# Dequantised feed-forward weights turned by VectorE's 32x32 block transpose instead of TensorE

## The chip, the cores and the metric

The kernel runs on one core of one Trainium2 chip. The metric is the time of one execution on the device in microseconds (us). An execution of the kernel before took 3075.28 us (median of 3 runs, 3073.91 to 3076.26).

## The reference

The program is a chain of four transformer blocks on `x` of shape (8, 128, 512). Each block adds an attention and then a feed-forward to the residual, each behind a layer norm:

```
x = x + L0_xattn(layernorm(x), ctx, ...)    x = x + L0_ffn(layernorm(x), ...)
x = x + L1_xattn(layernorm(x), ctx, ...)    x = x + L1_ffn(layernorm(x), ...)
x = x + L2_xattn(layernorm(x), ctx, ...)    x = x + L2_ffn(layernorm(x), w1, w2, w3)
x = x + L3_xattn(layernorm(x), ctx, ...)    x = x + L3_ffn(layernorm(x), ...)
```

The change concerns the third feed-forward, whose weights are first rounded to the 16 values of NF4 in blocks of 64 (w1 and w2 are 1376 x 512, w3 is 512 x 1376):

```
def nf4_quant_dequant(w):
    flat = w.reshape(-1, 64)
    absmax = max(abs(flat), axis=1)
    idx = searchsorted(bounds, flat / where(absmax == 0, 1, absmax))
    return (NF4_CODE[idx] * absmax).reshape(shape)
dq1, dq2, dq3 = (nf4_quant_dequant(w) for w in (w1, w2, w3))
h = silu(x @ dq1.T) * (x @ dq2.T)
return h @ dq3.T
```

None of this depends on `x`, so the rounding can be done at any time before that feed-forward. A matmul on TensorE sums over the 128 partitions, so the kernel needs w1 and w2 with their 512 columns on the partitions, and w3 with its 1376 columns there. In memory all three have them along a row; they have to be turned.

## The kernel before

Tokens are handled in 8 batches of 128, in two halves of four batches. TensorE (PE) multiplies, VectorE (DVE) and ScalarE (ACT) do the elementwise work, GpSimd (POOL) some of it, and SyncE's queue (SP) issues most DMAs. SP issues in order: a DMA that waits for its data, for a free buffer or for an earlier DMA holds up all DMAs behind it.

The first 1860 us are a loop over 128 attention *units* (heads times halves): 64 of the first attention (`Unit0`), then 64 of the third (`Unit2`). A unit projects keys and queries (L252), takes scores (L280) and a softmax, turns the probabilities, weighs the values (L297) and adds the output projection (L218, L219). The probabilities are turned by `blocks_turned` (L233): a VectorE transpose of 32x32 blocks within each quarter of the partitions (L240), a store of the result to DRAM (L242) and four loads that put the blocks in place (L245). Scores and turning run two units ahead of the weighing, projections three. Weights come on the SP queue into a pool of 20 buffers.

Beside the units runs side work, in `slot()` (L1145), which is called after each projection and at a few more points. A slot runs what a table holds for it (the first half's and second half's layer norms, the whole of the first feed-forward, the second attention and the second feed-forward: the *short stages*), and then so many *pieces* of the NF4 work as the rate allows:

```
NF4_PACE = ((2.1, 2.1), (0.9, 2.2), (0.2, 1.6), (1.6, 1.6))
...
due[0] += 0.0 if turning[0] else NF4_PACE[stage[0]][0 if table else 1]
```

The stage is the unit's number divided by 32; the second rate of a pair holds when the table is empty. On VectorE a piece is queued behind the last marked operation of the attention. A scheduler then settles the order of instructions on each engine from the order in which they are written and its own estimate of when each is ready.

The NF4 work is a generator over chunks of at most 128 x 512 elements (`nf4_items`). A `yield` ends a piece. `Rows` takes 128 rows of w1 or w2 (the last chunk 96): load, block maxima (L772), scaling (L776), 15 rounding steps, each a ScalarE activation (L739) and a VectorE operation (L748, L750), and scaling back (L780). w3 has 1376 = 21.5 blocks of 64 in a row, so blocks straddle rows: `PairMax` takes pairs of rows and finds the maxima (L809), and `Pairs` rounds the same pairs, 256 columns of each row at a time (scaling L837, once for each row of the pair). Each chunk is turned in the middle of the next one, by `turn`: up to four PE transposes into PSUM (L787 for `Rows`, L856 for `Pairs`), a ScalarE copy out (L789, L859) and stores to DRAM tensors `d1`, `d2`, `d3` (L790, L860). The third feed-forward, `l2_ffn`, loads its weights from these (about 1870 to 2100 us), and the fourth block follows.

`layernorm` (L174) normalises a batch; its last operation is L183. The result is turned on PE (L190) and copied to `xT`, the input of projections.

Of the kernel before, what the change touches and what calls it, by code (L numbers as in the profile page):

```python
# [11 lines left out]
F32 = mybir.dt.float32  # L12
# [11 lines left out]
P = 128  # L24
# [38 lines left out]
def kernel(ctx: ExitStack, tc: tile.TileContext, a, out):  # L63
# [107 lines left out]
    neg2 = keep.tile([P, B, P], BF16, name="neg2")  # L171
    cs = [keep.tile([P, 2, 512], F32, name=f"cs{hf}") for hf in range(2)]

    def layernorm(st, b):  # L174
        stats = st.small(6, "st")
        V.bn_stats(stats, x[b])
        mv = st.small(2, "mv")
        V.bn_aggr(mv, stats)
        rs = st.small(1, "rs")
        V.tensor_scalar(rs, mv[:, 1:2], 1e-5, None, ALU.add)  # L180
        inv_sqrt(rs, [P, 1])
        h = st.wide("h")
        V.tensor_scalar(h, x[b], mv[:, 0:1], rs, ALU.subtract, ALU.mult)  # L183
        return h

    def transposed(st, src):
# [566 lines left out]
    def nf4_scales(ri, am):  # L753
# [2 lines left out]
        V.tensor_add(ri, ri, am)  # L756
        V.reciprocal(ri, ri)

    class Rows:

        def __init__(self, name, dst, hc):
            self.name, self.dst, self.hc, self.n = name, dst, hc, min(P, FF - hc * P)

        def load(self):
            self.w = nfp.tile([P, 512], F32, tag="nw", name="nw")
            load(self.w[:self.n], a[self.name][self.hc * P:self.hc * P + self.n, :])

        def work(self):
            n, w = self.n, self.w
            wb = w.rearrange("p (k e) -> p k e", e=64)[:n]  # L770
            am = nfp.tile([P, 8], F32, tag="am", name="am")
            V.tensor_reduce(am[:n], wb, AX.X, ALU.max, apply_absolute_value=True)  # L772
            ri = nfp.tile([P, 8], F32, tag="ri", name="ri")
            nf4_scales(ri[:n], am[:n])
            yield
            V.tensor_tensor(wb, wb, along(ri[:n], 64), ALU.mult)  # L776
            yield
            dq = nfp.tile([P, 512], F32, tag="dq", name="dq", bufs=1)
            yield from nf4_round(dq[:n], w[:n])
            V.tensor_tensor(wb, dq.rearrange("p (k e) -> p k e", e=64)[:n], along(am[:n], 64), ALU.mult)  # L780
            yield

        def turn(self, st):
            n, hc = self.n, self.hc
            tp = st.tp()
            for c in range(DC):
                T.transpose(tp[:, c, :n], self.w[:n, c * P:(c + 1) * P], ident[:n, :n])  # L787
            wt = nfp.tile([P, 4, P], F32, tag="wt", name="wt", bufs=1)
            S.copy(wt[:, :, :n], tp[:, :, :n])  # L789
            nc.sync.dma_start(self.dst[:, :, hc * P:hc * P + n], wt[:, :, :n])  # L790

    class PairMax:
        def __init__(self, c, k):
# [7 lines left out]
        def work(self):  # L803
            k, nb = self.k, self.nb
            if k == 0:
                pair["am"] = nfp.tile([P, 43, 2], F32, tag="am3", name="am3", bufs=1)
            am = pair["am"]
            wb = self.w.rearrange("p (k e) -> p k e", e=64)[:, :nb, :]
            V.tensor_reduce(am[:, k:k + nb, 0], wb, AX.X, ALU.max, apply_absolute_value=True)  # L809
            yield  # L810
            if k + nb == 43:
                V.tensor_copy(am[:, :, 1], am[:, :, 0])
                ri = nfp.tile([P, 86], F32, tag="ri3", name="ri3", bufs=1)
                amf = am.rearrange("p k t -> p (k t)")
                nf4_scales(ri, amf)
                pair["amr"] = amf.rearrange("p (r k) -> p r k", r=2)
                pair["rir"] = ri.rearrange("p (r k) -> p r k", r=2)
                yield

        def turn(self, st):  # L820
            pass

    class Pairs:
        def __init__(self, c, hc):
            self.c, self.hc, self.nw = c, hc, min(2 * P, FF - hc * P)

        def load(self):
            nw, hc = self.nw, self.hc
            self.w = nfp.tile([P, 512], F32, tag="nw", name="nw")
            load(self.w[:, :2 * nw].rearrange("p (r h) -> p r h", r=2),  # L830
                 a["L2_ffn_w3"].rearrange("(c p r) h -> c p r h", c=2, r=2)[self.c, :, :, hc * P:hc * P + nw])

        def scale(self, dst, src, f):
            ks = slice(self.hc * 4, self.hc * 4 + self.nw // 32)
            for r in range(2):
                d, s = (t[:, r * self.nw:(r + 1) * self.nw].rearrange("p (k e) -> p k e", e=32) for t in (dst, src))
                V.tensor_tensor(d, s, along(f[:, r, ks], 32), ALU.mult)  # L837

        def work(self):
            w, nw = self.w, self.nw  # L840
            self.scale(w, w, pair["rir"])
            yield
            dq = nfp.tile([P, 512], F32, tag="dq", name="dq", bufs=1)
            yield from nf4_round(dq[:, :2 * nw], w[:, :2 * nw])
            self.scale(w, dq, pair["amr"])
            yield

        def turn(self, st):
            nw, hc, c = self.nw, self.hc, self.c
            tp = st.tp()  # L850
            wt = nfp.tile([P, 4, P], F32, tag="wt", name="wt", bufs=1)
            ns = [min(P, nw - j) for j in range(0, nw, P)]
            for i, n in enumerate(ns):
                for r in range(2):
                    o = r * nw + i * P
                    T.transpose(tp[:n, 2 * i + r, :], self.w[:, o:o + n], ident)  # L856
            for i, n in enumerate(ns):
                wd = wt[:n, 2 * i:2 * i + 2, :].rearrange("p r q -> p (r q)")
                S.copy(wd.rearrange("p (q r) -> p r q", r=2), tp[:n, 2 * i:2 * i + 2, :])  # L859
                nc.sync.dma_start(d3[hc + i, :n, c * 2 * P:(c + 1) * 2 * P], wd)  # L860

    pair = {}

    def nf4_items(st):
        chunks = [Rows(name, dst, hc) for name, dst in (("L2_ffn_w1", d1), ("L2_ffn_w2", d2)) for hc in range(NHC)]
        for c in range(2):
            chunks += [PairMax(c, k) for k in range(0, 43, 8)]
            chunks += [Pairs(c, hc) for hc in range(0, NHC, 2)]
        chunks[0].load()
        for k, chunk in enumerate(chunks):  # L870
            lag = 0 if isinstance(chunk, PairMax) else 5
            for i, _ in enumerate(chunk.work()):
                if i == lag:
                    if k > 0:
                        chunks[k - 1].turn(st)
                    if k + 1 < len(chunks):
                        chunks[k + 1].load()
                yield
        chunks[-1].turn(st)


    def l2_ffn(st, hf, f2, xT):
# [219 lines left out]
    with ExitStack() as early:  # L1102
# [24 lines left out]
        def put(i, f, *args):  # L1127
            table.setdefault(i, []).append((f, args))

        items = nf4_items(side)  # L1130
        now, due = [0], [0.0]

        def slot():
# [12 lines left out]
            while table:  # L1146
                slot()

        def norm_pieces(i, box, b, get):

            def norm():
                box[b] = layernorm(side, b)

            def turn():
                S.copy(get()[:, :, cols(b)], transposed(side, box[b]))

            put(i, norm)
            put(i + 1, turn)
# [114 lines left out]
        for u, unit in enumerate(units):  # L1273
            stage[0] = u // (4 * NG)
            turning[0] = 8 * NG - 4 <= u < 8 * NG
            if u == 3:
                l0_half(1)
            if u in (4 * NG - 3, 8 * NG - 3, 12 * NG - 3):
                drain()
            if not unit.far:  # L1280
                unit.turn()
            if u + 3 < len(units):
                for f in units[u + 3].pieces():
                    f()
                    slot()
            if u + 2 < len(units):
                units[u + 2].score()
                if units[u + 2].far:
                    units[u + 2].turn_far()
            unit.weigh()  # L1290
            if isinstance(unit, Unit2):
                slot()
            unit.after(units, u)
            if u in (4 * NG - 1, 8 * NG - 1):
                short_stages((u + 1) // (4 * NG) - 1)
            if u == 12 * NG + 1:
                now[0] = 0
                xT.append(xt_tile())
                for b in batches(0):
                    norm_pieces(2 * b, {}, b, lambda: xT[0])  # L1300
        for _ in items:
            pass
    ps = ctx.enter_context(tc.tile_pool(name="ps2", bufs=1, space=PSUM))
# [2 lines left out]
    xT.append(xt_tile())  # L1306
    xT3 = []

    def late_norm(b, get):
        box = {}  # L1310
        return [lambda: box.setdefault("h", layernorm(late, b)),
                lambda: S.copy(get()[:, :, cols(b)], transposed(late, box["h"]))]

    with tc.tile_pool(name="f2", bufs=2) as f2:
        extra = [f for b in batches(1) for f in late_norm(b, lambda: xT[1])]
        for _ in l2_ffn(late, 0, f2, xT[0]):
            if extra:
                extra.pop(0)()
# [166 lines left out]
```

## Time and profile before

| what | value |
|---|---|
| time, median of 3 runs | 3075.28 us (3073.91 to 3076.26) |
| time of the profiled execution | 3075.35 us |
| its span in the profile | 3073.6 us, mean granted PE clock 0.998 |
| busy: PE, DVE, ACT, POOL | 3041.6, 1876.2, 1373.3, 384.4 us |
| DMA | 427.42 MB, 139 GB/s in the mean |
| NF4 chunk loads by SP | 46, first at 14.4 us, last at 1746.9 us |
| PE transposes of chunks | 88 (L787) and 44 (L856), 99.3 to 1795.5 us |

The span is one execution, from the first to the last instruction that the hardware profiler recorded. Busy time is the time in which an engine had an instruction running. PE's matmuls are pipelined: the next one starts before the end of the one before, so the time that a matmul costs is read from the distance of starts, and its listed duration is longer. PEld is PE's loading of the stationary operand, which overlaps. A group line reads: line, engine, operation, output from inputs, sizes, count | busy us, mean ns of one | idle time of the engine just before, and what ended it.

### The profile page before, as it was taken

The numbers are of one execution on the slowest core, as the hardware profiler recorded it, in microseconds if no ns is written. First come the engines' busy times: TensorE is split into PE (matmuls) and PEld (weight loads), VectorE is DVE, ScalarE is ACT, GpSimd is POOL, SyncE is SP. The second block draws the span as 40 slices with busy tenths as digits, with TensorE's granted clock in tenths as the row PEclk, the third lists the DMA queues.
The fourth block names the chain that finished last, engine by engine and source line by source line (L and its number), as shares of the span: only waits on it lengthen the run. The fifth ranks groups of instructions, "written<-read, shape, count | busy, mean of one in ns | idle before, by whom it ended". The sixth has DMA issues, their size and how long they took to land.

```text
span 3073.6 us, 35109 instructions
## 1 busy us (share of the span) xinstructions
PE 3041.6 (99%) x10720; PEld 1668.8 (54%) x10724; DVE 1876.2 (61%) x3765; ACT 1373.3 (45%) x3856; POOL 384.4 (13%) x490
## 2 busy tenths in 40 slices
PE   9999999999999999999999999999999999999999
PEld 4555555544444565555555554445656656555554
DVE  5666666657766566898889862214554555555544
ACT  4555555435654433665556641003343433433332
POOL 2000000101211021332111110001111111111110
PEclk9999999999999999999999999999999999999999
DMA  6434343336654533665344342223565645655540
GB/s 216 127 113 120 120 134 116 110 100 181 177 157 126 153 111 92 179 188 171 117 139 129 122 121 77 78 73 117 165 193 165 193 161 176 189 173 168 175 126 14
DMA packets 425564, 427.42 MB, mean 139 GB/s; under 512 B 40160, under 2 KB 315296, under 8 KB 424864
## 3 DMA queue, kind: packets, MB, share of 16 engines
q1 hardware_dynamic: 391200, 348.60, 37.3%
q10 hardware_dynamic: 23040, 41.95, 4.4%
q0 software_dynamic: 11136, 34.61, 3.8%
q8 instruction: 87, 1.43, 0.2%
q14 instruction: 101, 0.83, 0.1%
HBM read 308.70 MB, written 116.33 MB: 138 GB/s over the span
## 4 chain that ended last, share of the span: by engine, by line
PE 47%; DVE 3%; ACT 1%; issue 0%; POOL 0%; DVEq 0%; ACTq 0%; POOLq 0%
PE po L218 7%; PE tp L945 7%; PE mm L968 7%; PE mm L903 5%; PE mm L218 4%; PE pv L1028 4%; PE sc L1005 3%; PE mm L252 3%; PE mm L912 2%; PE mm L1096 1%; PE mm L1084 1%; PE pv L297 1%; DVE dq L750 1%; PE sc L280 1%; PE mm L682 1%; PE mm L672 1%
## 5 line engine op out<-in xcount | busy, mean ns | idle before, releaser
L252 PE MATMUL mm<-xT,w 128*128 128x512 f32 x1024 | 466.0, 597 | 2.3 <-DVE rot L662 2.3
L218 PE MATMUL mm<-w,o 128*128 128x512 f32 x1024 | 465.1, 598 | 1.6 <-ACT o L299 1.5
L739 ACT ACTIVATE ind<-nw,bounds 128x512 f32<-128x512 f32 (+2 forms) x510 | 350.0, 703 | 235.5 <-DVE dq L750 162.8
L750 DVE SCALAR_TENSOR_TENSOR dq<-ind,dq 128x512 f32<-128x512 f32 (+2 forms) x476 | 333.1, 700 | 23.0 <-ACT ind L739 8.2
L252 PEld LDWEIGHTS mm<-xT,w 128*128 128x128 f32 x1024 | 190.1, 191 | 220.5 <-issue 211.7
L218 PEld LDWEIGHTS mm<-w,o 128*128 128x128 f32 x1024 | 189.7, 191 | 220.4 <-issue 208.5
L213 ACT ACTIVATE s<-s,nm 128x128 f32<-128x128 f32 x512 | 198.3, 388 | 101.9 <-DVE nm L271 101.2
L968 PE MATMUL mm<-w,xT 128*128 128x512 f32 x512 | 233.9, 592 | 0.0
L218 PE MATMUL po<-w,o 128*128 128x512 f32 x512 | 233.2, 594 | 0.0
L252 PE MATMUL mm<-ctxT,w 128*128 128x512 f32 x512 | 230.4, 593 | 0.8 <-ACT ctxT L1249 0.8
L384 PE MATMUL mm<-w,ctxT 128*128 128x512 f32 x512 | 230.4, 593 | 0.0
L213 ACT ACTIVATE p<-sc,nm,rq 128x256 f32<-128x256 f32 x256 | 141.1, 562 | 114.6 <-DVE nm L1010 110.9
L219 DVE TENSOR_TENSOR x<-x,mm 128x512 f32<-128x512 f32 x128 | 87.1, 680 | 143.1 <-PE mm L218 142.8
L280 PEld LDWEIGHTS sc<-k,q 128*128 128x128 f32 x1024 | 131.7, 192 | 49.8 <-issue 44.6
L159 POOL TENSOR_TENSOR rs<-rs,mhalf 128x1 f32<-128x1 f32 x64 | 38.2, 598 | 950.6 <-DVE rs L180 510.0
L218 PEld LDWEIGHTS po<-w,o 128*128 128x128 f32 x512 | 96.3, 190 | 110.6 <-issue 102.8
L384 PEld LDWEIGHTS mm<-w,ctxT 128*128 128x128 f32 x512 | 94.7, 190 | 108.0 <-issue 107.1
L903 PE MATMUL mm<-xT,w 128*128 128x512 f32 (+1 forms) x352 | 152.5, 592 | 0.8 <-DVE x L219 0.8
L299 ACT COPY o<-pv 128x512 f32<-128x512 f32 x128 | 74.3, 580 | 173.8 <-PE pv L297 173.7
L1009 DVE TENSOR_REDUCE nm<-sc 128x2 f32<-128x512 f32 x128 | 85.3, 674 | 103.1 <-PE sc L1005 102.8
L252 PEld LDWEIGHTS mm<-ctxT,w 128*128 128x128 f32 x512 | 93.4, 190 | 99.1 <-issue 97.8
L968 PEld LDWEIGHTS mm<-w,xT 128*128 128x128 f32 x512 | 97.0, 190 | 89.4 <-issue 84.7
(254 smaller groups left out, 4749.0 us busy)
## 6 DMA issues: line engine op xcount, KB each, us to landing
w<-in_l_wq SPq DMA_DIRECT2D x128, 256.0 KB
w<-in_l_wo SPq DMA_DIRECT2D x128, 256.0 KB
far<-tb SPq DMA_DIRECT2D x125, 256.0 KB
pt<-far SPq DMA_DIRECT2D x500, 64.0 KB
far<-tb SPq DMA_DIRECT2D x60, 512.0 KB
pt<-far SPq DMA_DIRECT2D x240, 128.0 KB
far<-tb SPq DMA_DIRECT2D x63, 384.0 KB
pt<-far SPq DMA_DIRECT2D x252, 96.0 KB
```

The costliest lines, as they stand in the source:

```text
L213: S.activation(dst(h), src(h), AF.Exp, bias=negm[:, h:h + 1], scale=by, accum_out=su[:, h:h + 1])
L218: T.matmul(mm, lhsT=o(h), rhs=wo[h], start=h == 0, stop=h == 3)
L252: T.matmul(mm, lhsT=w[:, c, :], rhs=xT[:, c, :], start=c == 0, stop=c == DC - 1)
L280: T.matmul(sc[:, i, :], lhsT=self.q[:, i * P:(i + 1) * P], rhs=k[:, i * P:(i + 1) * P], start=True, stop=True)
L384: T.matmul(mm, lhsT=ctxT[:, c, toks(self.hf * HALF + i)], rhs=grp.wv[c], start=c == 0, stop=c == DC - 1)
L739: S.activation(ind, w, AF.Relu, bias=bounds[:n, i:i + 1], scale=(down + up)[i][1])
L750: V.scalar_tensor_tensor(dst, ind, step, dst, ALU.min, ALU.subtract if i == len(down) else ALU.add)
L903: T.matmul(mm[:n, :], lhsT=w[c][:, j * P:j * P + n], rhs=xT[:, c, :], start=c == 0, stop=c == DC - 1)
L945: T.matmul(it.kv[:, s, :], lhsT=lhsT, rhs=it.wkv[c // 2][:, c % 2, :], start=c == 0, stop=c == DC - 1)
L968: T.matmul(mq, lhsT=self.xT[it.hf][:, c, cols(it.b)], rhs=it.wq[c], start=c == 0, stop=c == DC - 1)
L1005: T.matmul(sc[:, i, :], lhsT=it.qT[2 * j + i], rhs=it.kT, start=True, stop=True)
L1028: T.matmul(pv, lhsT=it.v[:, j, :], rhs=it.pts[j], start=j == 0, stop=j == 1)
```

## The change

The 132 PE transposes of dequantised weights, the 44 ScalarE copies behind them and the `turn` methods go. In their place each chunk ends with one VectorE transpose of 32x32 blocks and one store, as a piece of its own. Such a transpose only turns blocks within a quarter of the partitions. So that this is enough, a chunk is put together differently:

- A chunk of w1 or w2 holds, on quarter q of the partitions, 32 rows at a time of the columns 128q to 128q + 127, for the row groups m, m + 11, m + 22 and m + 33 (three of them for m = 10). It is loaded by four DMAs of 32 partitions, in runs of 512 bytes. After turning, partition 32q + i and chunk b hold column 128q + 32b + i. The sum over the 512 dimensions is thus taken in another order, and the input of the third feed-forward is put in that order too: `layernorm` with `quarters=True` writes its result permuted (8 calls, L183).
- A chunk of w3 (`Columns`, replacing `Pairs`) holds, on quarter q, 32 output dimensions at a time of the columns from 32(11q + m). There are 11 such chunks, each of 512 columns (the last on 96 partitions), instead of 12. Their loads are four DMAs (three for the last) in runs of 512, 256 or 128 bytes. The blocks' maxima are needed in that arrangement: both `PairMax` sequences now run first, their maxima go to a DRAM tensor `far_am`, and `columns_scales` loads them back arranged, in four DMAs with runs of up to 11 elements.
- The hidden dimension of 1376 follows the same order in `d1`, `d2` and `d3`.

Pieces of a `Rows` chunk go from 17 to 18, of a w3 chunk from 16 to 17. The small tiles `am` and `ri` have one buffer instead of two.

The core of the diff:

```diff
 class Rows:
     def load(self):
         self.w = nfp.tile([P, 512], F32, tag="nw", name="nw")
-        load(self.w[:self.n], a[self.name][self.hc * P:self.hc * P + self.n, :])
+        src = a[self.name].rearrange("(g j) (a e) -> a j g e", j=32, a=4)
+        for q in range(4):
+            load(self.w[32 * q:32 * q + 32, :self.n].rearrange("p (k e) -> p k e", e=P), src[q, :, self.m::NHC, :])
     def work(self):
         ...
         yield
-    def turn(self, st):
-        n, hc = self.n, self.hc
-        tp = st.tp()
-        for c in range(DC):
-            T.transpose(tp[:, c, :n], self.w[:n, c * P:(c + 1) * P], ident[:n, :n])
-        wt = nfp.tile([P, 4, P], F32, tag="wt", name="wt", bufs=1)
-        S.copy(wt[:, :, :n], tp[:, :, :n])
-        nc.sync.dma_start(self.dst[:, :, hc * P:hc * P + n], wt[:, :, :n])
+        wt = nfp.tile([P, 512], F32, tag="wt", name="wt", bufs=1)
+        V.transpose(wt[:, :n].rearrange("p (n j) -> p n j", j=32), w[:, :n].rearrange("p (k b i) -> p b k i", b=DC, i=32))
+        load(self.dst[:, :, self.m * P:self.m * P + n // 4], wt[:, :n].rearrange("p (b h) -> p b h", b=DC))
+        yield
 class PairMax:
     ...
         if k + nb == 43:
             V.tensor_copy(am[:, :, 1], am[:, :, 0])
-            ri = nfp.tile([P, 86], F32, tag="ri3", name="ri3", bufs=1)
-            ...
+            load(far_am[self.c], am.rearrange("p k t -> p (k t)"))
             yield
+def columns_scales():
+    am = pair["amr"] = nfp.tile([P, 16, NHC], F32, tag="amr", name="amr", bufs=1)
+    G.memset(am[96:128, :, NHC - 1:NHC], 1.0)
+    src = far_am.rearrange("c p (r g) -> (c p r) g", r=2).rearrange("(k j) g -> j k g", j=32)
+    for q in range(4):
+        n = min(NHC, 43 - NHC * q)
+        load(am[32 * q:32 * q + 32, :, :n], src[:, :, NHC * q:NHC * q + n])
+    ri = pair["rir"] = nfp.tile([P, 16, NHC], F32, tag="rir", name="rir", bufs=1)
+    nf4_scales(ri, am)
+    yield
+class Columns:
+    def load(self):
+        self.w = nfp.tile([P, 512], F32, tag="nw", name="nw")
+        w3 = a["L2_ffn_w3"].rearrange("(k j) h -> j k h", j=32)
+        for q in range(self.n // 32):
+            o = 32 * (NHC * q + self.m.start)
+            load(self.w[32 * q:32 * q + 32, :self.nw].rearrange("p (k e) -> p k e", e=32 * self.nm), w3[:, self.k, o:o + 32 * self.nm])
+    def work(self):
+        ...
+        wt = nfp.tile([P, 512], F32, tag="wt", name="wt", bufs=1)
+        V.transpose(wt[:n, :nw].rearrange("p (n j) -> p n j", j=32), w[:n, :nw].rearrange("p (k m i) -> p m k i", m=self.nm, i=32))
+        load(d3[self.m, :n, 32 * self.k.start:32 * self.k.stop].rearrange("m p d -> p m d"), ...)
+        yield
 def nf4_items():
-    for c in range(2):
-        chunks += [PairMax(c, k) for k in range(0, 43, 8)]
-        chunks += [Pairs(c, hc) for hc in range(0, NHC, 2)]
+    chunks += [PairMax(c, k) for c in range(2) for k in range(0, 43, 8)]
+    for m, nm in ((0, 4), (4, 4), (8, 2), (10, 1)):
+        chunks += [Columns(k, 16 // nm, m, nm) for k in range(0, 16, 16 // nm)]
     ...
-                if k > 0:
-                    chunks[k - 1].turn(st)
 def layernorm(st, b, quarters=False):
     ...
-    V.tensor_scalar(h, x[b], mv[:, 0:1], rs, ALU.subtract, ALU.mult)
+    src, dst = x[b], h
+    if quarters:
+        src, dst = src.rearrange("p (a b i) -> p a b i", a=4, i=32), dst.rearrange("p (b a i) -> p a b i", a=4, i=32)
+    V.tensor_scalar(dst, src, mv[:, 0:1], rs, ALU.subtract, ALU.mult)
```

More of the change, by code (lines that the diff above doesn't have):

```diff
@@ L172, with layernorm @@
     cs = [keep.tile([P, 2, 512], F32, name=f"cs{hf}") for hf in range(2)]
-    def layernorm(st, b):
+    def layernorm(st, b, quarters=False):
         stats = st.small(6, "st")
@@ L757, in nf4_scales, with groups, __init__ @@
         V.reciprocal(ri, ri)
+    def groups(m):
+        return 4 if m < NHC - 1 else 3
     class Rows:
-        def __init__(self, name, dst, hc):
-            self.name, self.dst, self.hc, self.n = name, dst, hc, min(P, FF - hc * P)
+        def __init__(self, name, dst, m):
+            self.name, self.dst, self.m, self.n = name, dst, m, groups(m) * P
         def load(self):
             self.w = nfp.tile([P, 512], F32, tag="nw", name="nw")
-            load(self.w[:self.n], a[self.name][self.hc * P:self.hc * P + self.n, :])
+            src = a[self.name].rearrange("(g j) (a e) -> a j g e", j=32, a=4)
+            for q in range(4):
+                load(self.w[32 * q:32 * q + 32, :self.n].rearrange("p (k e) -> p k e", e=P), src[q, :, self.m::NHC, :])
@@ L768, in work @@
         def work(self):
             n, w = self.n, self.w
[L770 to L774, printed above, removed]
+            nb = n // 64
+            wb = w[:, :n].rearrange("p (k e) -> p k e", e=64)
+            am = nfp.tile([P, 8], F32, tag="am", name="am", bufs=1)
@@ L775, in work @@
+            V.tensor_reduce(am[:, :nb], wb, AX.X, ALU.max, apply_absolute_value=True)
+            ri = nfp.tile([P, 8], F32, tag="ri", name="ri", bufs=1)
+            nf4_scales(ri[:, :nb], am[:, :nb])
             yield
-            V.tensor_tensor(wb, wb, along(ri[:n], 64), ALU.mult)
+            V.tensor_tensor(wb, wb, along(ri[:, :nb], 64), ALU.mult)
             yield
             dq = nfp.tile([P, 512], F32, tag="dq", name="dq", bufs=1)
-            yield from nf4_round(dq[:n], w[:n])
-            V.tensor_tensor(wb, dq.rearrange("p (k e) -> p k e", e=64)[:n], along(am[:n], 64), ALU.mult)
+            yield from nf4_round(dq[:, :n], w[:, :n])
@@ L781, in work @@
+            V.tensor_tensor(wb, dq[:, :n].rearrange("p (k e) -> p k e", e=64), along(am[:, :nb], 64), ALU.mult)
             yield
-        def turn(self, st):
-            n, hc = self.n, self.hc
-            tp = st.tp()
-            for c in range(DC):
-                T.transpose(tp[:, c, :n], self.w[:n, c * P:(c + 1) * P], ident[:n, :n])
-            wt = nfp.tile([P, 4, P], F32, tag="wt", name="wt", bufs=1)
-            S.copy(wt[:, :, :n], tp[:, :, :n])
-            nc.sync.dma_start(self.dst[:, :, hc * P:hc * P + n], wt[:, :, :n])
+            wt = nfp.tile([P, 512], F32, tag="wt", name="wt", bufs=1)
@@ L794 @@
+            V.transpose(wt[:, :n].rearrange("p (n j) -> p n j", j=32), w[:, :n].rearrange("p (k b i) -> p b k i", b=DC, i=32))
+            load(self.dst[:, :, self.m * P:self.m * P + n // 4], wt[:, :n].rearrange("p (b h) -> p b h", b=DC))
+            yield
+    far_am = dram.tile([2, P, 86], F32, name="far_am")
     class PairMax:
@@ L812, in work @@
                 V.tensor_copy(am[:, :, 1], am[:, :, 0])
-                ri = nfp.tile([P, 86], F32, tag="ri3", name="ri3", bufs=1)
[L814 to L817, printed above, removed]
-                yield
[L820 to L825, printed above, removed]
+                load(far_am[self.c], am.rearrange("p k t -> p (k t)"))
@@ L827, in load, with __init__ @@
+    class Columns:
+        def __init__(self, k, nk, m, nm):
+            self.k, self.m, self.nk, self.nm = slice(k, k + nk), slice(m, m + nm), nk, nm
+            self.n, self.nw = 32 * groups(m), nk * nm * 32
         def load(self):
-            nw, hc = self.nw, self.hc
             self.w = nfp.tile([P, 512], F32, tag="nw", name="nw")
-            load(self.w[:, :2 * nw].rearrange("p (r h) -> p r h", r=2),
-                 a["L2_ffn_w3"].rearrange("(c p r) h -> c p r h", c=2, r=2)[self.c, :, :, hc * P:hc * P + nw])
+            w3 = a["L2_ffn_w3"].rearrange("(k j) h -> j k h", j=32)
+            for q in range(self.n // 32):
+                o = 32 * (NHC * q + self.m.start)
+                load(self.w[32 * q:32 * q + 32, :self.nw].rearrange("p (k e) -> p k e", e=32 * self.nm), w3[:, self.k, o:o + 32 * self.nm])
@@ L833, in scale @@
         def scale(self, dst, src, f):
[L834 to L837, printed above, removed]
+            d, s = (t[:self.n, :self.nw].rearrange("p (k m e) -> p k m e", k=self.nk, e=32) for t in (dst, src))
+            V.tensor_tensor(d, s, f[:self.n, self.k, self.m].unsqueeze(3).to_broadcast([self.n, self.nk, self.nm, 32]), ALU.mult)
@@ L839, in work @@
         def work(self):
-            w, nw = self.w, self.nw
+            w, n, nw = self.w, self.n, self.nw
+            if "amr" not in pair:
+                yield from columns_scales()
             self.scale(w, w, pair["rir"])
@@ L843, in work, with nf4_items @@
             dq = nfp.tile([P, 512], F32, tag="dq", name="dq", bufs=1)
-            yield from nf4_round(dq[:, :2 * nw], w[:, :2 * nw])
+            yield from nf4_round(dq[:n, :nw], w[:n, :nw])
             self.scale(w, dq, pair["amr"])
             yield
[L848 to L860, printed above, removed]
-    pair = {}
-    def nf4_items(st):
-        chunks = [Rows(name, dst, hc) for name, dst in (("L2_ffn_w1", d1), ("L2_ffn_w2", d2)) for hc in range(NHC)]
-        for c in range(2):
-            chunks += [PairMax(c, k) for k in range(0, 43, 8)]
-            chunks += [Pairs(c, hc) for hc in range(0, NHC, 2)]
+            wt = nfp.tile([P, 512], F32, tag="wt", name="wt", bufs=1)
+            V.transpose(wt[:n, :nw].rearrange("p (n j) -> p n j", j=32), w[:n, :nw].rearrange("p (k m i) -> p m k i", m=self.nm, i=32))
+            load(d3[self.m, :n, 32 * self.k.start:32 * self.k.stop].rearrange("m p d -> p m d"),
+                 wt[:n, :nw].rearrange("p (m d) -> p m d", m=self.nm))
+            yield
+    pair = {}
+    def nf4_items():
+        chunks = [Rows(name, dst, m) for name, dst in (("L2_ffn_w1", d1), ("L2_ffn_w2", d2)) for m in range(NHC)]
+        chunks += [PairMax(c, k) for c in range(2) for k in range(0, 43, 8)]
+        for m, nm in ((0, 4), (4, 4), (8, 2), (10, 1)):
+            chunks += [Columns(k, 16 // nm, m, nm) for k in range(0, 16, 16 // nm)]
         chunks[0].load()
@@ L872, in nf4_items @@
             for i, _ in enumerate(chunk.work()):
-                if i == lag:
-                    if k > 0:
-                        chunks[k - 1].turn(st)
-                    if k + 1 < len(chunks):
-                        chunks[k + 1].load()
+                if i == lag and k + 1 < len(chunks):
+                    chunks[k + 1].load()
                 yield
-        chunks[-1].turn(st)
     def l2_ffn(st, hf, f2, xT):
@@ L1128, in put @@
             table.setdefault(i, []).append((f, args))
-        items = nf4_items(side)
+        items = nf4_items()
         now, due = [0], [0.0]
@@ L1147, in drain, with norm_pieces @@
                 slot()
-        def norm_pieces(i, box, b, get):
+        def norm_pieces(i, box, b, get, quarters=False):
             def norm():
-                box[b] = layernorm(side, b)
+                box[b] = layernorm(side, b, quarters)
             def turn():
@@ L1299 @@
                 for b in batches(0):
-                    norm_pieces(2 * b, {}, b, lambda: xT[0])
+                    norm_pieces(2 * b, {}, b, lambda: xT[0], True)
         for _ in items:
@@ L1307, with late_norm @@
     xT3 = []
-    def late_norm(b, get):
+    def late_norm(b, get, quarters=False):
         box = {}
-        return [lambda: box.setdefault("h", layernorm(late, b)),
+        return [lambda: box.setdefault("h", layernorm(late, b, quarters)),
                 lambda: S.copy(get()[:, :, cols(b)], transposed(late, box["h"]))]
     with tc.tile_pool(name="f2", bufs=2) as f2:
-        extra = [f for b in batches(1) for f in late_norm(b, lambda: xT[1])]
+        extra = [f for b in batches(1) for f in late_norm(b, lambda: xT[1], True)]
         for _ in l2_ffn(late, 0, f2, xT[0]):
```

## The prediction

> **What bounds the kernel now.** I read the page's engine totals, then stretches of the span, then the timeline around the instructions that go away, then the waits of the DMA-issuing queue.
>
> The totals:
>
> ```profile
> PE 3041.6 (99%) x10720; PEld 1668.8 (54%) x10724; DVE 1876.2 (61%) x3765; ACT 1373.3 (45%) x3856; POOL 384.4 (13%) x490
> ```
>
> TensorE (PE) is idle for 3073.6 - 3041.6 = 32 us in all. Busy could still hide slack, as matmul ends are modelled, so I look at starts, in the first feed-forward-weight stretch:
>
> ```profile
> 606.64 3.60 PE L384 MATMUL mm<-w,ctxT 128*128 128x512 f32 x8
> 610.08 0.60 PE L787 MATMUL tp<-ident,nw 128*128 128x128 f32 x4
> 610.51 3.60 PE L218 MATMUL mm<-w,o 128*128 128x512 f32 x8
> ```
>
> (Columns: start, us, what.) Eight 512-column matmuls start 3.44 us apart, 0.43 each; the four transposes hold the engine from 610.08 to 610.51: 0.43 us for four, 0.107 each, not the 0.27 of the modelled duration. Nothing waits in between. Whatever is taken out of this stream is taken out of the time, as long as the others keep up. Whether they do, by stretches (us, then busy us of PE, PEld, DVE, ACT, POOL with counts, granted clock, DMA share, GB/s):
>
> ```profile
> 400.00:500.00 100.00, 100.00 (x303) 49.81 (x302) 62.88 (x115) 54.64 (x121) 0.00 (x0) 1.00 0.38 117
> 1200.00:1500.00 300.00, 288.60 (x1356) 159.40 (x1357) 262.04 (x443) 173.25 (x632) 89.33 (x118) 0.99 0.55 166
> 1500.00:1800.00 300.00, 297.14 (x1225) 175.49 (x1224) 258.87 (x449) 186.49 (x530) 52.05 (x39) 1.00 0.42 128
> 1800.00:1862.00 62.00, 61.70 (x245) 35.68 (x243) 27.68 (x46) 21.96 (x81) 6.35 (x5) 1.00 0.40 123
> ```
>
> At 400 PE is full and VectorE (DVE) has a third free. From 1200 to 1800 DVE is at 87%; there PE loses 11.4 and 2.9 us. This is the thin place. From 1800 DVE is at 45%.
>
> **The change part by part.**
>
> *Transposes on PE go.* 22 chunks of w1 and w2 (20 of four transposes, two of four 96-wide ones) and 12 of w3 (ten of four, two of two):
>
> ```profile
> L787 PE MATMUL tp<-ident,nw x88: 243/273/327, 99.3 to 1047.3; 128*128 128x128 f32 x80, 96*128 96x96 f32 x8
> L856 PE MATMUL tp<-ident,nw x44: 272/273/315, 1327.7 to 1795.5; 128*128 128x128 f32 x40, 128*96 128x128 f32 x4
> ```
>
> In starts: 20 x 0.43 + 2 x 0.33 (the timeline has 1047.09 to 1047.42) = 9.3; 10 x 0.43 + 2 x 0.21 = 4.7; one wait of 0.28 before an L856 transpose, seen in the timeline. Together **-14.2 us**, all on the bounding engine.
>
> *VectorE transposes come.* There are 33 in the changed program (30 of 128x512, two of 384 columns, one on 96 partitions). The nearest row is the attention's own turn, the same instruction, with the same four-dimensional reading in runs of 32:
>
> ```profile
> L240 DVE STREAM_TRANSPOSE tb<-s 128x512 f32<-128x512 f32 x125 | 88.5, 708 | 15.9 <-ACT s L700 13.3 <-DMA w<-in_l_wq 0.5
> L837 DVE TENSOR_TENSOR nw<-nw,ri 128x256 f32<-128x256 f32 x20 | 7.8, 420 | 0.5 <-DMA nw<-in_L_ffn_w 0.4
> L776 DVE TENSOR_TENSOR nw<-nw,ri 128x512 f32<-128x512 f32 x20 | 13.8, 688 | 0.4
> ```
>
> 33 x 0.70 = +23 us of DVE. Against it: 48 half-width scalings of w3 (40 x 0.42 + 8 x 0.25 = 18.8) become 22 whole ones (22 x 0.69 = 15.2): -3.6. The twelve w3 chunks (ten whole, two of 192 columns) become eleven: each whole one rounds in 0.47 + 14 x 0.714 = 10.5 us, a narrow one in about 7.3, so 119.6 to 115.5: -4. The last w1 and w2 chunks are 384 columns on 128 partitions instead of 512 on 96, at about 0.55 instead of 0.68 each: -4. Net about +11 us, on 1876.
>
> [...] I take -14.2. [...]
>
> Nor does DVE get denser: the rounding is fed in pieces at a fixed rate per slot of attention work. A w1 chunk was 17 pieces in about 13.0 us, now 18 in 13.7: 0.76 per piece both ways; a w3 chunk 0.76 and now 0.74. Following the slot rates through the code, the pieces (580, now 598) end at unit 123 of 128 instead of unit 120, some 35 us later, still before the feed-forward loads must be complete, in the stretch with DVE at 45%. In the order of the built program the last store stands between the same weight loads of the third feed-forward. Cost 0; if it came after the stage's end, up to those 35 us.
>
> *ScalarE:* 44 copies out of PSUM go (22 x 0.58 + 22 x 0.39 = -21 us), off the path: 0. They also leave the three PSUM buffers of the side work; no wait shows there, so 0.
>
> *The SP queue* gets 92 more DMAs (1943 to 2035): each chunk's load becomes four of 64 KB. An issue took 0.38 to 0.57 us, so 35 to 50 us more of issuing over 1800 us. What is queued behind: attention weights and the return of the turned probabilities. Its waits (us in total, times, longest):
>
> ```profile
> SPq L121 <- PE mm L252: 334.1, 133, 7.4
> SPq L790 <- ACT wt L789: 9.4, 10, 2.5
> SPq L242 <- DVE tb L240: 406.8, 144, 65.5
> ```
>
> It mostly stands waiting for PE to free a weight buffer, so it is ahead of PE: 0. A store now waits at its head for a DVE transpose rather than an ACT copy: 33 times up to the 2.8 us that an L242 store waits on average (406.8 / 144), instead of 16 us in all. Loads of this size and with runs of 512 B are what the turned probabilities come back by ("pt<-far", 500 of 64 KB, with 3.9 us to landing); a chunk is loaded a chunk ahead (45 us), so landing time is hidden.
>
> *The scales of w3* make a round trip through DRAM once: two stores, four loads in runs of 44 B, then three small operations at once behind them in DVE's order, and the softmaxes behind those. No row has such runs; between 0 (fully ahead) and about 8 us (two landings at the longest seen, 7.8 us, with half covered by SP's lead), nearest the 3.9 us landing, of which PE with two units of lead should see nothing. I take 0. *The layer norm in quarters:* eight L183 with a different output order, 0.6 us each; -0.1 to +0.4 each, bounded by an operation's own size; they feed transposes two slots later: 0.
>
> *The start.* In the program's order the context transposes of batch 4 move behind later matmuls, since eight small loads now stand in front. Before, PE waited for that tile:
>
> ```profile
> 30.88 0.90 PE L190 MATMUL tp<-ident,h 128*128 128x128 f32 x4 [1.82 <-DMA h<-in_ctx]
> 31.00:35.00 4.00, 4.00 (x9) 0.57 1.06 416
> ```
>
> The second row is a stretch again, PE alone (after the busy time the granted clock, 0.57): the 16 matmuls after the gap took 8.52 us instead of 6.87. [...] Yet a gap of 2.48 us at 1401 left the clock at 1.00. The next tile on PE there is ready at 30.15 (last L342), so 0.7 us of the gap go surely, and the slow clock perhaps: between 0.7 and 2.4, unless the delayed loads bring a new gap (+2). I take **-1.5**.
>
> *Sum:* against the profiled execution's 3075.35 (span 3073.6 and 1.75 around it): -14.2 - 1.5 = -15.7, so 3059.7; that run is within 0.1 us of the median of 3075.28. I say 3060.
>
> **The rivals.**
> *A, the w3 part is not paid out.* From 1200 to 1800 the L856 transposes partly fill time in which PE would wait for DVE. For it: DVE at 87%, 14 us of PE idle there. Against: the idle time sits in some ten gaps and one transpose only had a wait. Then 9.3 of the 14.2 and little else: 3075.3 - 9.3 = 3066.
> *B, more than counted.* Some gaps from 1200 to 1500 go too, as the maxima of w3 (0.68 us of DVE, no ACT work) now fall where rounding fell: 19.8 us of rounding and 2.9 of scaling stood there on DVE. Half the 11.4 us of gaps: 3060 - 6 = 3054; with their slow clock 3051.
> *C, slower: the store at the head of the SP queue.* SP takes things in order; a store held by a late DVE transpose holds up probabilities and weights behind it, and PE starves from 1200 on, where DVE is 87% busy. Each gap of 1.5 to 2.5 us costs up to 1.65 more in clock. It decides once a hold exceeds SP's lead, which the 7 us waits for PE put near 7 us: 11 w3 stores at 2 us each give back 22, so 3082. Against: L242 waits of that kind are everywhere today and PE has one gap from them (2.5 us). With the DRAM round trip's 8 us and half of C it comes to no change.
>
> **How the numbers follow.** A measurement of this kernel tells about 0.2%, 6 us, from no change. Forecast, 3056 to 3064: 0.57. A, 3064 to 3069: 0.14. B, 3050 to 3056: 0.13. Around no change: 0.08. C, over 3081: 0.08. Faster 0.84, same 0.08, slower 0.08. The range leaves out C, no change and a little of B: 3051 to 3069.
>
> **What would show it.** PE loses its 132 nw transposes and its busy time falls by about 14 us to 3027; 33 DVE transposes of about 0.7 us stand in their place; PE's idle time stays at 28 to 33 us. Wrong if the transposes take 1 us or more, if PE idle from 1200 to 1862 grows past 15 us, or if SP's waits for wt pass 60 us with PE gaps behind them.

## The result and the profile after

The changed kernel took 3064.03 us (median of 7 runs, 3062.04 to 3068.18) against 3074.91 for the kernel before (7 runs): ratio 0.9966, 95% interval 0.9957 to 0.9975. Measured once more later it gave 3066.91 against 3074.65, ratio 0.9974 (0.9965 to 0.9983). It is faster by 8 to 11 us, inside the stated range; the central forecast was 15.

Span and totals of the page after:

```profile
span 3063.2 us, 34925 instructions
PE 3029.4 (99%) x10592; PEld 1656.1 (54%) x10592; DVE 1894.9 (62%) x3754; ACT 1352.1 (44%) x3797; POOL 386.5 (13%) x491
```

PE's busy time fell by 12.2 us, its count by 128 for 132 transposes (a few records can be missing), and its idle time is 33.8 us instead of 32.0. The transposes as they now run (operation, count, ns min/median/max, first and last start):

```profile
L796 DVE STREAM_TRANSPOSE wt<-nw x22: 572/704/714, 86.8 to 1161.3; 128x512 f32<-128x512 f32 x20, 128x384 f32<-128x384 f32 x2
L866 DVE STREAM_TRANSPOSE wt<-nw x11: 668/702/714, 1493.1 to 1819.2; 128x512 f32<-128x512 f32 x10, 96x512 f32<-96x512 f32 x1
```

They cost what the attention's own row said. The stretches after (the last two columns DMA share and GB/s, the one before them the granted clock), first the changed kernel's, then those of the kernel before at the same borders:

```profile
1180.00:1480.00 300.00, 287.01 (x1346) 158.81 (x1345) 257.75 (x432) 157.38 (x594) 86.90 (x117) 0.98 0.59 170
1480.00:1870.00 390.00, 383.30 (x1502) 219.53 (x1502) 325.75 (x524) 229.05 (x630) 64.75 (x50) 1.00 0.41 122
```

```profile
1180.00:1480.00 300.00, 288.60 (x1356) 159.46 (x1357) 252.19 (x429) 162.15 (x598) 89.10 (x119) 0.99 0.53 159
1480.00:1870.00 390.00, 386.46 (x1567) 226.28 (x1566) 308.90 (x533) 221.15 (x647) 63.37 (x50) 1.00 0.41 126
```

Both differ where the prediction put a zero. PE was busy 1.6 and 3.2 us less (0.6 of the 3.2 is a gap of the kernel before that lies just behind the border), and DVE worked 5.6 and 16.9 us more. Most of the 16.9 stands late. In two parts, the kernel before and then the changed one:

```profile
1480.00:1700.00 220.00, 218.60 (x906) 129.56 (x905) 191.64 (x330) 136.76 (x382) 38.27 (x29) 1.00 0.44 134
1480.00:1700.00 220.00, 215.73 (x868) 125.42 (x868) 196.46 (x314) 137.53 (x373) 39.90 (x30) 1.00 0.41 124
```

Up to 1700 DVE has 4.8 us more, behind it 12.

A busy PE can be a slow PE (in the changed kernel it was busy all through 1381.79 to 1388.62, at a granted clock of 0.50), so the time is split in three. I read busy time and granted clock of PE in stretches of 4 us up to 3052. *Idle* is the sum of 4 minus busy, *slow clock* the sum of 4 times (1 minus clock). What is left of the span is PE's work at full speed, together with some 5 us of idle time behind 3052 that all four profiles have. There are two profiles of each kernel; the second ones (3070.0 us for before, 3063.8 for the changed kernel) are from the last experiments below. Idle + slow clock, in us:

| stretch (us) | before | before, 2nd | changed | changed, 2nd |
|---|---|---|---|---|
| 0 to 960 | 4.3 + 1.7 | 5.2 + 0 | 3.5 + 0 | 3.6 + 0 |
| 960 to 1180 | 5.6 + 1.7 | 4.7 + 0 | 4.1 + 1.7 | 3.7 + 0 |
| 1180 to 1480 | 11.4 + 3.4 | 12.6 + 1.7 | 13.0 + 6.8 | 11.9 + 10.3 |
| 1480 to 1872 | 4.1 + 0 | 4.3 + 0 | 6.7 + 0 | 6.8 + 0 |
| 1872 to 3052 | 1.5 + 0 | 1.3 + 0 | 1.3 + 0 | 1.3 + 0 |
| work at full speed | 3039.9 | 3040.2 | 3026.1 | 3026.2 |

The last line is the change's own worth: -13.8 and -14.0 us in the two pairs. Another 4.0 and 2.6 us come before 1180. Against that stand 5 to 8 us from 1180 to 1480, most of it slow clock, and 2.5 us of waits from 1480 to 1872.

What such a wait is after 1480. In the changed kernel, around a unit that begins a new group of heads (start, us, what, and in brackets the idle time before and what ended it):

```profile
1629.31 0.68 DVE L663 TENSOR_TENSOR k<-mm,cs 128x512 f32<-128x512 f32 x1
1630.01 0.69 DVE L665 TENSOR_TENSOR rot<-mm,cs 64x512 f32<-64x512 f32 x1
1630.72 0.68 DVE L666 TENSOR_TENSOR rot<-mm,cs 64x512 f32<-64x512 f32 x1
1631.45 1.98 PE L256 MATMUL mm<-xT,w 128*128 128x512 f32 x4 [0.54 <-DVE rot L666]
```

The query projection needs the PSUM buffer that the rope's last operation reads. In the kernel before the same place reads:

```profile
1508.10 0.68 DVE L659 TENSOR_TENSOR k<-mm,cs 128x512 f32<-128x512 f32 x1
1508.80 0.69 DVE L661 TENSOR_TENSOR rot<-mm,cs 64x512 f32<-64x512 f32 x1
1509.51 0.68 DVE L662 TENSOR_TENSOR rot<-mm,cs 64x512 f32<-64x512 f32 x1
1510.22 3.17 DVE L750 SCALAR_TENSOR_TENSOR dq<-ind,dq 128x512 f32<-128x512 f32 x3
1510.24 3.27 PE L252 MATMUL mm<-xT,w 128*128 128x512 f32 x7
```

There the rope ended at 1510.19 and PE went on without a gap. It was just in time, 0.05 us ahead, so anything that makes DVE half a microsecond later shows. Before, two waits on the rope stood from 1500 on, 2.3 us in all; now there are seven of this kind and two short ones elsewhere, 4.5 us.

The slow clock comes behind gaps: in the first profiles of the two kernels, without the first and last 10 us, all seven stretches of half clock begin behind 3.41 us in which PE was idle for 1.3 to 2.7 us. The changed kernel at 1381, PE and DVE:

```profile
1378.85 1.96 DVE L244 STREAM_TRANSPOSE tb<-s 128x1024 f32<-128x1024 f32 x2
1379.09 0.65 PE L561 MATMUL pv<-pt,vt 128*32 128x128 f32 x16
1380.72 0.65 DVE L701 SCALAR_TENSOR_TENSOR s<-sc,neg 128x512 f32<-128x512 f32 x1
1381.52 1.80 PE L284 MATMUL sc<-k,q 128*128 128x128 f32 x8 [1.79 <-DVE s L701]
```

The gap and the stretches behind it, PE alone (length, busy us and count, then the granted clock):

```profile
1378.38:1381.79 3.41, 1.62 (x20) 1.00 0.09 36
1381.79:1385.20 3.41, 3.41 (x12) 0.50 0.79 272
1385.20:1388.62 3.42, 3.42 (x6) 0.50 0.90 206
```

The clock is half for 6.8 us, so the gap of 1.8 us costs another 3.4. In the kernel before the scheduler had put the score read between the two transposes:

```profile
1389.83 1.23 DVE L240 STREAM_TRANSPOSE tb<-s 128x1024 f32<-128x1024 f32 x1
1390.99 0.64 DVE L697 SCALAR_TENSOR_TENSOR s<-sc,neg 128x512 f32<-128x512 f32 x1
1391.56 0.68 DVE L240 STREAM_TRANSPOSE tb<-s 128x512 f32<-128x512 f32 x1
1391.78 1.13 PE L280 MATMUL sc<-k,q 128*128 128x128 f32 x8
```

No wait there, and full clock. A little later the kernel before has a gap that the changed one has not, also at full clock:

```profile
1401.30 0.91 PE L297 MATMUL pv<-pt,v 128*128 128x128 f32 x6 [2.48 <-DMA pt<-far]
```

These transposes are the attentions' own; the change only moved what stands around them, and the order came out otherwise.

### The profile page after: what moved, and what is told of

Read it like the earlier page. It is cut to its first block, busy times and chain, and to the rows that moved or that the text cites. A ratio compares the mean times of both kernels' runs of the same rounds, so it can differ in the third digit from the quotient of the medians.

```text
span 3063.2 us, 34925 instructions
## 1 busy us (share of the span) xinstructions
PE 3029.4 (99%) x10592; PEld 1656.1 (54%) x10592; DVE 1894.9 (62%) x3754; ACT 1352.1 (44%) x3797; POOL 386.5 (13%) x491
## 4 chain that ended last, share of the span: by engine, by line
PE 82%; DVE 12%; ACT 3%; issue 2%; DMA 1%; POOL 0%; SPq 0%; DVEq 0%; ACTq 0%; POOLq 0%
PE mm L256 17%; PE mm L222 11%; PE mm L388 7%; PE po L222 7%; PE tp L950 7%; PE mm L973 7%; PE mm L908 5%; PE pv L1033 4%; PE sc L1010 4%; PE mm L917 2%; PE sc L284 2%; PE pv L301 2%; DVE dq L753 2%; ACT s L217 1%; DVE tb L244 1%
```

## The experiments

All times are medians, each against runs of the kernel before on the same chip. For comparison, the changed kernel's ratios are 0.9966 and 0.9974.

**Each half alone.** `e1_rows_only`: the new `Rows` in the kernel before, with neighbouring row groups so that the hidden dimension keeps its order, and the old `Pairs`. Here is how its load differs from that of the changed kernel:

```diff
-                load(..., src[q, :, self.m::NHC, :])
+                load(..., src[q, :, 4 * self.m:4 * self.m + groups(self.m), :])
```

> Only w1 and w2 are turned on VectorE (their chunks take neighbouring groups of rows, so the hidden dimension keeps its order); w3 is rounded and turned as before, on TensorE. Counted: 22 groups of PE transposes go, 9.3 us, and the start gains 3 us as in the changed kernel. Theory V (VectorE is full between 1200 and 1860 us, so the w3 part is given back there in new PE waits): 3062 to 3063, as fast as the full change or 1 to 2 us faster. Theory M (what costs is the new order of the w3 work, maxima first and their way through DRAM): 3062 to 3063 too. Theory Q (the 92 more DMAs on the SP queue, 66 of which are here, cost it): 3064 or more.

Measured: 3068.6 us, ratio 0.9972 (0.9960 to 0.9983), 7.6 us below before. That is slower than V and M had it and lies in the range of Q, which a later run tests.

`e2_cols_only`: the new `PairMax` and `Columns` with the old `Rows` and its PE transposes; the rows' load is new:

```diff
+            src = a[self.name].rearrange("(g j) d -> g j d", j=32)
+            for k in range(groups(self.m)):
+                load(self.w[32 * k:32 * k + 32], src[self.m + NHC * k])
```

> Only w3 is turned on VectorE, in the new order with the maxima first; w1 and w2 are turned on TensorE as before, their rows loaded in the new order of the hidden dimension (four DMAs of 32 rows). Counted on TensorE alone: -4.9 us, 3070. Theory V: the gain is given back, 3074 to 3077. Theory M: the same 3074 to 3077. Without any such cost: 3070.

Measured: 3074.15 us, ratio 0.9993 (0.9985 to 1.0001): at most some 4 us, about 2, in the range that V and M share. Split as above, e1 has 8.7 us less full-speed work than before and e2 4.3, close to the counts of 9.3 and 4.9. Both lose more than the kernel before from 1180 to 1480: 19.3 and 17.8 us against 14.8. So the loss is not tied to one half. e1 has it without any of the new w3 work, which speaks against the maxima's new order as its cause. e2 also gets through the start faster: a projection that starts at 47.7 us in the kernel before (46.8 in its second profile) starts at 44.7, as in the changed kernel. In e2 the loads are split but w1 and w2 are still turned on PE, so the gain at the start belongs to the loads' division.

**Without the transposes of w3.** `e3_no_w3_turn` stores w3 as it is, not turned:

```diff
-            self.scale(w, dq, pair["amr"])
-            ...
-            V.transpose(wt[:n, :nw].rearrange("p (n j) -> p n j", j=32), w[:n, :nw].rearrange("p (k m i) -> p m k i", m=self.nm, i=32))
+            wt = nfp.tile([P, 512], F32, tag="wt", name="wt", bufs=1)
+            self.scale(wt, dq, pair["amr"])
```

> The changed kernel without the eleven VectorE transposes of w3: the last scaling writes the tile that is stored, so that the stored w3 is not turned; all else as in the changed kernel. It takes 7.7 us of VectorE out of 1450 to 1840 us. Theory V: 2 to 5 us faster than the changed kernel, 3059 to 3062, with fewer PE waits after 1500. Theory M: no faster, 3063 to 3065.

Measured: 3065.28 us, ratio 0.9963 (0.9949 to 0.9977), as the changed kernel; 6.9 us idle from 1480 to 1870, where it has 6.7. Theory V in its narrow form falls: the eleven transposes by themselves are not what costs. Nor is it the sum of DVE's work, which is back near that of the kernel before (191.6 us, 193.3 in its second profile):

```profile
1480.00:1700.00 220.00, 215.90 (x879) 126.26 (x878) 192.62 (x309) 138.20 (x379) 38.77 (x30) 1.00 0.42 126
```

The waits on the rope are still nine, 4.6 us. Neither half alone has them: e1 has 2.2 us of such waits and e2 2.3, as the kernel before.

**The maxima early.** `e4_maxima_early` moves the two `PairMax` sequences between w1 and w2.

> The changed kernel with the two sequences of w3 maxima (and their stores) put between the chunks of w1 and those of w2, so that they run in the first attention, and the load of the scales long after their stores; the rounding of w2 takes their place at 1000 to 1450 us. Theory M: 3 to 5 us faster than the changed kernel, 3059 to 3061. Theory V: no faster, 3063 to 3067, as the same VectorE work per slot stands in the full stretch, with longer pieces than the maxima.

Measured: 3066.86 us, ratio 0.9975 (0.9964 to 0.9986), no faster. Theory M falls. The trip through DRAM shows up as one 1.2 us wait of SP in the changed kernel.

**More DMAs.** `e7_loads_doubled` splits each quarter's load into two of 16 partitions.

> The changed kernel with each quarter's load split into two DMAs of 16 partitions: 128 more DMAs on the SP queue, the same bytes in the same runs. Theory Q (the added loads on SP cost part of the gain): 3 us or more slower than the changed kernel, 3067 to 3070. Theories C and D: the same as the changed kernel within 1.5 us.

Measured: 3066.43 us, ratio 0.9972 (0.9962 to 0.9983). The intervals overlap: no cost of 128 more DMAs is clear of noise, and idle time and slow clock up to 3052 are the same, 36.9 us against 37.1. A cost of some 4 us is not excluded by the times alone, but theory Q has no support. SP's waits for the transposed tile were small in the changed kernel (us in total, times, longest):

```profile
SPq L113 <- DVE wt L866: 8.6, 7, 2.9
SPq L113 <- DVE wt L796: 2.9, 4, 1.3
```

**How full VectorE is.** Here the amount of NF4 work from 1000 us on was changed, not its form. `e5_pace` and `e6_pace_before`, with the turning of the changed kernel and of the kernel before:

```diff
-        NF4_PACE = ((2.1, 2.1), (0.9, 2.2), (0.2, 1.6), (1.6, 1.6))
+        NF4_PACE = ((2.7, 2.7), (1.15, 2.75), (0.0, 1.0), (1.0, 1.0))
```

> The changed kernel with other rates of NF4 pieces: 2.7 for 2.1, (1.15, 2.75) for (0.9, 2.2) in the first attention, where VectorE has a third free, none during the second short stages and 1.0 for 1.6 in the third attention. 503 of 598 pieces are done by unit 64 instead of 393. In the traces so far the changed kernel loses 19.8 us to PE waits and slow clock from 1180 to 1480 us and 6.7 from there to 1870 (before: 14.8 and 4.1). Theory D (VectorE's fill by NF4 work from 1200 on sets these losses): both fall, together by 5 to 10 us, 3055 to 3060. Theory C (the losses of 1180 to 1480 come from the short stages' own chains, and how much the clock adds is chance; only the waits on the rope after 1480 come from NF4 work): 2 to 4 us faster than the changed kernel, 3061 to 3063. Against both: new waits in the first attention, 3065 or more.

> The kernel before with the same new rates. Theory D: it gains as the changed kernel does, 4 to 9 us, 3066 to 3071, so the rates are worth the same with either way of turning. Theory C: 1 to 3 us, 3072 to 3074. If the transposes on PE mattered for the waits, the gain here would be clearly smaller than in the changed kernel.

Measured: e5 3054.2 us, ratio 0.9934 (0.9921 to 0.9948), faster than the changed kernel and than before. e6 3073.34 us, ratio 0.9993 (0.9984 to 1.0002). So at the new rates the two ways of turning differ by 19.1 us, more than the 14.2 that were counted; up to 1872 the profiles of e5 and e6 have 24.1 and 32.4 us of idle time and slow clock. The stretches of e5, columns as before:

```profile
1180.00:1480.00 300.00, 291.33 (x1359) 160.31 (x1359) 249.84 (x417) 157.92 (x603) 89.46 (x118) 0.98 0.54 161
1480.00:1870.00 390.00, 388.33 (x1516) 222.78 (x1515) 254.71 (x424) 175.68 (x540) 57.29 (x49) 1.00 0.37 114
```

From 1480 on DVE has 71 us less to do than in the changed kernel, and PE is idle for 1.7 instead of 6.7: the rope waits are gone. From 1180 to 1480 the idle time fell from 13.0 to 8.7, but the slow clock is the same 6.8. In e6 idle fell from 11.4 to 9.2 and from 4.1 to 3.3 in the two stretches, while slow clock rose by 3.4 and 1.7: it has the 1.28 us gap before the scores, as at 1381 above, and slow clock behind it. That is where its gain went. D's forecast for the time of e6 (3066 to 3071) fails and C's holds. For e5 it is the other way round: 26.5 us of losses from 1180 on fell to 17.2, by 9.3, inside the 5 to 10 that D gave, and the time is below both ranges.

**No w3 work at all.** `e8_no_w3_work` leaves out maxima, scales, rounding and turning of w3; its chunks are only loaded and stored.

> The changed kernel without the work on w3: its maxima, scales, rounding and turning are left out (its chunks are only loaded and stored). About 165 us of VectorE and 120 us of ScalarE go from 1000 to 1840 us. Theory D: the losses of 1180 to 1480 and of 1480 to 1870 fall from 26.5 us to under 12, so 3050 or less. Theory C: those after 1480 go (5 us), those of the short stages stay at 15 to 20: 3057 to 3061.

Measured: 3055.81 us, ratio 0.9937 (0.9924 to 0.9951). Idle from 1480 to 1870 is 1.4 us, but from 1180 to 1480 it is 11.7 + 6.8. This is theory C's split, with a time 1 us below its range: the waits behind 1480 go with w3's work, and what is lost in the short stages is lost nearly as much without it.

**All NF4 work early.** `e9_pace_all_early` uses (3.2, 3.2), (1.4, 3.3), (0.0, 1.0), (1.0, 1.0).

> The changed kernel with rates of 3.2 and (1.4, 3.3) in the first attention, so that nearly all NF4 pieces are done by unit 64 and none of them runs in the third attention. Theory C (what is lost from 1180 to 1480 is the short stages' own chains with the slow clock behind their gaps; NF4 work causes only the rope waits after 1480, which e5_pace already took down to 1.7 us): within 2 us of e5_pace's 3054, with 15 to 19 us still lost from 1180 to 1480. Theory D (NF4 work on VectorE sets all of it): another 5 us or more faster, 3049 or less. If the first attention cannot hold that much (VectorE there at 73% in e5_pace, some 80% here): new waits before 1000 us, 3057 or more.

Measured: 3060.43 us, ratio 0.9957 (0.9944 to 0.9971), slower than e5, so neither C's nor D's time but that of the third case. From 1180 to 1480 16.6 us are lost, within C's range and above e5's 15.5; from 1480 on 1.4. What is new stands early: a wait of 1.53 us at 120 and 4.3 us instead of 2.2 at 970. The first attention does not hold that much; e5's rates are near what it takes.

**Once more.** The two kernels again, for a second profile.

> The changed kernel once more, for a second profile and more times: 3062 to 3066. If the part of the loss that is slow clock is chance, it differs from the first profile's 8.5 us by a multiple of about 1.7 us while the instruction order and the count of gaps are the same; if it is set by the program, it is 8.5 us again.

> The kernel before once more, for a second profile: about 3075. Its first profile lost 6.8 us to slow clock, 1.7 of it at the start and 3.4 from 1180 to 1480 us. If slow clock is chance, these shares move between profiles by steps of about 1.7 us; if it is set by the program, they are the same again, and the 3.4 us more of the changed kernel from 1180 to 1480 are a cost of the change.

Measured: 3066.91 us for the changed kernel (11 runs), 3071.76 for before (one run, near the lowest of the 15 others on that chip, 3071.54 to 3079.06). In the profiles the full-speed work is the same to 0.3 us, idle the same to 1.4, while slow clock went from 8.5 to 10.3 and from 6.8 to 1.7: a change of one step and of three. So part of it is chance. Part is not. Each run lists its span and its mean granted clock; span times (1 minus clock) averages 6.8 us over 54 runs of the kernel before and 10.0 us over 18 of the changed one (8.3 in the first seven, 11.2 in the later eleven). The difference of 3.3 us is uncertain by about 1.3. And behind the gap at 1381 the changed kernel has slow clock in both profiles; before has none there in either, with no gap in the first and one of 0.8 us in the second.

## Why the prediction was right or wrong

- *Transposes on PE, -14.2:* right; -13.8 and -14.0 in full-speed work. Reading their cost from the distance of starts (0.107 us) and not from the listed 0.27 decided this.
- *VectorE transposes, 0.70 each:* the durations were right (medians of 0.704 and 0.702 us), and so was taking the -14.2 of PE although DVE's net is a plus: from 400 to 500 the kernel before had PE busy for all of the 100 us and DVE free for 37, and with the change no new wait stands in the first 960 us. The net of +11 us of DVE was too low; the page has +18.7. By lines, the transposes are +23.0 and the last chunks of w1 and w2 -3.7 (23.9 to 20.2), both as said, but two savings on w3 did not come. Its scalings fell by 0.2 (16.4 to 16.2) instead of 3.6: the half-width ones had been priced at their listed 0.42 us each, though two in a row take 0.76. Its rounding fell by nothing instead of 4: the whole chunks took 0.721 us an operation instead of 0.714, and the new last one 0.795.
- *ScalarE -21, SP's stores and loads, the DRAM trip, the quarters' layer norm at 0:* right as far as the runs show; ScalarE fell by 21.2, SP waited 11.5 us for transposed tiles, the layer norm's last operation keeps its median of 546 ns, and e7 shows no cost of the loads. (The 3.9 us to landing is that of the 128 loads of 128 KB that POOL issued; for SP's loads of 64 KB the profile has none.)
- *The start, -1.5:* the right mechanism, slightly under. The wait fell from 1.82 (2.70 in the second profile) to 1.18, and the slow clock that the first profile had behind it is gone: -2.5 and -1.6 before 960. A further 1 to 1.5 us came from 960 to 1180 and was not foreseen.
- *The step that failed* is "Nor does DVE get denser ... Cost 0", and with it rival B, which had the gaps from 1200 shrinking. DVE had 4.8 us more from 1480 to 1700 and 12 more from there to 1870, where the NF4 work now ends later (last transpose at 1819 instead of 1796 us). The waits on the rope, which had been just in time, grew from 2.3 to 4.5 us, most of the 2.5 us of new idle time. That these waits come from the NF4 work is shown: with less of it (e5) or without w3's (e8) there are none. That the sum of DVE's work makes them is not: e3 has the sum of the kernel before and keeps the waits. Which operation delays the rope stays open. The test I set for being wrong, PE idle above 15 us from 1200 to 1862, was met, at 19.7; it stood at 14.6 before already, so it was a thin test.
- *The term that was missing* is the slow clock. The prediction used it for the start and for pricing rival C, and gave it no place in the sum for 1180 to 1480, where ten gaps stood and each may cost 1.7 us or 3.4 more. It grew by 3.4 and 8.6 us there, with the idle time within 1.6 us of before; over all runs the clock cost 3.3 us more. The total fell inside the range because that was wide enough to hold rival A, not because these two terms, some 6 us together, were foreseen.
- *The rivals:* the first time, 3064.03, lies on the border of the forecast and A's range, the second, 3066.91, in A's, but not only for A's reason: e2 shows w3's half worth 2 instead of 4.9 us, and e1 shows the other half losing too. C, the store at the head of SP's queue, did not occur.

What stays open, besides the rope: why the slow clock from 1180 to 1480 was 1.7 to 3.4 us in the two profiles of before and 5.1 to 10.3 in all eleven others, e6 with its PE transposes among them. By the clock that every run lists the difference is smaller: 6.8 us over the 54 runs of the kernel before, 8.3 over 66 of the nine other kernels, 10.0 for the changed one. The place at 1381 is the common part: in all eleven half clock begins between 1379 and 1397 us, for 3.4 or 6.8 us. In eight it follows the gap before the scores, in e1, e2 and e4 a gap of 2.3 to 2.9 us before the weighing, which both profiles of before passed at full clock. Why the gap before the scores arises in so many variants was not tested; nor were the single buffers of `am` and `ri` alone.

## What to carry to other kernels

Where one engine is full, price a removed instruction by the distance of starts on that engine; here that held to 0.4 us in 14. Then ask of the engine that takes the work in which stretch its last operation is just in time for the full one: here neither the idle share nor the sum of work showed it (from 1480 to 1700 e3 has the sum of the kernel before, 192.6 us against 191.6, and keeps its waits of 4.6 us), while the gap of 0.05 us behind the rope at 1510 did. Side work that feeds on rates should be put where its engine is free before its form is changed: with the rates moved to the first attention, the same change was worth 19 us instead of 8 to 11, while the rates alone were worth about 2.

## What the hardware showed

Gaps of about 1 to 3 us on PE cost more than themselves in some places and not in others: the 1.79 us at 1381 in the changed kernel were followed by 6.8 us of half clock, the 2.48 us before 1401.30 in the kernel before by none. Half clock came in stretches of 3.41 us or twice that, which is 1.7 or 3.4 us lost: the totals of slow clock move in steps of 1.7 (1.7, 3.4, 6.8, 8.5, 10.3). Within each of the thirteen profiles, all such stretches begin at whole multiples of 3.413 us from each other. In the changed kernel they begin at 968.78, 1245.26 and 1381.79 us, which is 81 and 40 steps apart, in the kernel before at 31.15, 980.06, 1259.95 and 1314.56 us, 278, 82 and 16 steps apart. Steps of this length, carried through the whole span, make a grid of cells for each profile. The gap at 1381 lay whole in one cell, the first of the three rows shown above. The longer one before 1401.30 in the kernel before was divided by a border of its grid, 1.08 us and 1.40 (PE alone):

```profile
1396.48:1399.89 3.41, 2.33 (x6) 1.00 1.00 221
1399.89:1403.30 3.41, 2.00 (x11) 1.00 0.31 93
1403.30:1406.72 3.42, 3.42 (x23) 1.00 0.57 211
```

Counted over the thirteen profiles, without their first and last 10 us, half clock followed 23 of the 24 full-clock cells in which PE was idle for 2 us or more, 21 of 58 with 1.2 to 2 us, and 2 of 130 with 0.6 to 1.2 us. The grid lies differently in the two profiles of the changed kernel, with a border at 1378.38 in one and at 1379.58 in the other; that chance comes in there is my reading, not shown by a run. What makes a stretch twice as long, or a cell with little idle time enough, is not shown.
